# A graph layer with segment maximum on one core: the bytes of the slot stage's temporaries and of the accumulator change places

## The chip, the core and the metric

The kernel runs on one core of one Trainium2 chip. The metric is the device time of one execution in microseconds. The kernel before takes 754.3 us (median of 3 runs, 753.62 to 754.97). One more execution was recorded by the hardware profiler; it took 746.02 us, and all the rows below are from it.

The engines are called as in the profile: PE multiplies matrices, DVE (VectorE) and ACT (ScalarE) work on tiles elementwise, POOL (GpSimd) issues the indirect loads, SP (SyncE) issues most of the direct ones.

## What is computed

```python
e   = relu((x[dst] - x[src]) @ theta_w.T + theta_b + x[src] @ phi_w.T + phi_b)   # one row per edge
out = segment_max(e, dst, num_segments=6250)        # 0 for a node with no edge
y   = layernorm(x + out)
```

There are 6250 nodes of 256 float32 and 100000 edges, sorted by dst. Since the dst part is the same for all edges of a node, the kernel computes b = x (phi − theta)' once for every node, takes for every node the maximum of b over its sources, adds a = x theta' + biases, and applies relu, residual and normalisation.

## The kernel before, in words

**Stages.** The search (`search_edges`, L621) finds where the nodes' edges lie; a branch (L653) would sort the edges if they weren't sorted. B's stage (L710 to L784) loads the weights and biases (L719, L722), prepares them (L726 to L740), loads x in 13 shares (L775), transposes (L747) and multiplies (L759) on PE with copies on ACT (L749, L762), and stores b in DRAM as `b_rows`. The end stage (from L1292) multiplies x by theta, joins it with the maxima and normalises.

**Two ways to the maxima.** The first 1130 nodes are done by 146 gather steps: POOL loads one row for each of 128 partitions by an indirect DMA (L512), DVE folds it into the running maximum (L688). 48 of these rows come from x and are multiplied in B's stage (`x_group`, L764), 98 come from `b_rows`. They lie in a ring of 6 tiles `g` of 8 rows.

The other 5120 nodes are done mostly by one-hot matmuls. `b_rows` is cut into 17 slots of 383 rows; for each node and slot a choice (`choice`, L997, on DVE) names one row of the slot, and `wanted` (L1024) stores these names as `chosen_rows` in DRAM, two slots at a time. `slot_terms` (L1039) loads a slot's rows into `raw` (one buffer), and makes two terms of them: a cast on ACT (L1053) and the difference on DVE (L1054). `slot_part` (L1056) does one slot for one chunk of 1024 nodes: it loads `want` from `chosen_rows` (L1061), makes one-hot rows of it, one block of 128 rows on DVE (L1065, once `dve_hots` is 1) and the others on ACT (L1067, L1068), does 24 matmuls (L1075; 8 in the last slot) in two halves, and joins each half with the accumulator `acc`: a copy on ACT for slot 0 (L1084), a maximum on DVE (L1086) for the other 16 slots. There are 85 such parts.

What a slot can't name goes to a list: `list_pieces` (L1167) packs the left-over edges to the front of a table of 1440 words in moves by powers of two (L1200, L1203), tags them (L1208, L1209), stores them in DRAM as `list_words` (L1210), loads them again from where each partition's run begins (three gathers `dst_w`, by `gather_run`, L521) and makes `list_src` and caps of them (L1221 to L1235). Then 232 list gathers (`gather_2`, L1260) go through POOL, and DVE folds them in by L688 too, and stores of `maxima` follow.

**What sets the order.** The program is written stage by stage, but a planner puts the instructions of each engine in the order in which it expects them to be ready. It must keep data dependences, and also those by place: a tile whose pool was opened where an earlier pool had been closed can't be written before the earlier tiles' readers are done. `behind_in_order` adds an order of two instructions without a wait; POOL's gathers are held in the written order in this way (`in_turn`, L506), and the list's L688 behind the latest L1086 (L694).

**What the change touches.** The pool `accs` with `acc` (L703, L704) is opened ahead of B's stage, the pools `work` (heads, owner, `hot_1` and other small tiles) and `slots` (`raw`, `terms`, `want`, `hot`, `rows`) behind it (L786, L787), where the pools of B's stage, `prep`, `x_in` and `b_out`, have just been closed. The sort's and the search's pools were closed ahead of these (L648, L662). In `slot_terms` the three or four row loads (L1045, L1047, L1051) are issued without any order of their own.

Of the kernel before, what the change touches and what calls it, by code (L numbers as in the profile page):

```python
# [40 lines left out]
FP = mybir.dt.float32  # L41
# [11 lines left out]
P = 128  # L53
# [45 lines left out]
def flat(t, offset, ap):  # L99

    return bass.AP(tensor=t.tensor, offset=t.offset + offset, ap=ap)
# [326 lines left out]
def gnn_kernel(ctx: ExitStack, tc: tile.TileContext, x, src, dst, theta_w, theta_b, phi_w, phi_b, out):  # L428
    nc = tc.nc
    N, D = x.shape  # L430
    E = src.shape[0]
    T = -(-E // P)
    KC = D // P
    OWN = P * TILES
# [20 lines left out]
    body = ctx.enter_context(ExitStack())  # L455
    ps_misc = body.enter_context(tc.tile_pool(name="ps_misc", bufs=2, space=PSUM))

    b_rows = dram.tile([N, D], FP, name="b_rows")
    maxima_1 = dram.tile([P * T1 + 1, D], FP, name="maxima_1")
    maxima_2 = dram.tile([P * LIST + 1, D], FP, name="maxima_2")  # L460
# [12 lines left out]
    def shares(width):  # L473

        main = ((1, Q1), (2, TILES))
        return [LAST] + [(part, j, min(width, n - j)) for part, n in main for j in range(0, n, width)]

    def node_rows(t, part, j0, n):
        if (part, j0, n) == LAST:
            return t[P * Q1 : N1, :].rearrange("p (o d) -> p o d", o=1)  # L480
        base, tiles = (0, Q1) if part == 1 else (N1, TILES)
        return flat(t, (base + j0) * D, [[tiles * D, P], [D, n], [1, D]])

    def present(t, part, j0, n):
        return t[: LEFT1 if (part, j0, n) == LAST else P, :n, :]
# [16 lines left out]
    def behind_in_order(one, name, reason):  # L502
        after = mybir.DependencyInfo(mybir.DependencyClass.NoSync, mybir.DependencyReason.DATA)
        tc.add_manual_dep(one.ins, name, after, reason=reason)
# [49 lines left out]
    whole = [[E // P, P], [1, E // P]]  # L554
    rest = [[E % P, 1], [1, E % P]]
# [142 lines left out]
    def run_1(i, gathers=()):  # L698
        t0, n = groups[i]
        run(1, ring_tiles[i], n, caps_1, t0, maxima_1t[:, t0 : t0 + n, :], gathers)  # L700


    acc_pool = body.enter_context(tc.tile_pool(name="accs", bufs=1))  # L703
    acc = acc_pool.tile([P, KC, OWN], FP, name="acc")  # L704

    weights = const.tile([P, KC, 2, D], FP, name="weights")

    bias_terms = const.tile([P, D], FR, name="bias_terms")
# [1 line left out]
    with (  # L710
        tc.tile_pool(name="prep", bufs=1) as prep,
        tc.tile_pool(name="x_in", bufs=4) as x_in,
        tc.tile_pool(name="b_out", bufs=2) as b_out,
        tc.tile_pool(name="ps_t", bufs=3, space=PSUM) as ps_t,
        tc.tile_pool(name="ps_b", bufs=3, space=PSUM) as ps_b,
    ):
        w_in = prep.tile([P, 2, KC, D], FP, name="w_in")
        for i, w in enumerate((phi_w, theta_w)):
            nc.sync.dma_start(w_in[:, i], w.rearrange("(c p) k -> p c k", p=P))  # L719
        biases = prep.tile([P, 2, D], FP, name="biases")  # L720
        for i, b in enumerate((theta_b, phi_b)):
            nc.sync.dma_start(biases[:, i, :], flat(b, 0, [[0, P], [1, D]]))  # L722
        bias = prep.tile([P, D], FP, name="bias")
        rest = prep.tile([P, D], FP, name="rest")
        high_part = prep.tile([P, D], FR, name="high_part")
        nc.vector.tensor_add(bias, biases[:, 0, :], biases[:, 1, :])  # L726
        nc.vector.tensor_copy(high_part, bias)
        nc.vector.tensor_tensor(rest, bias, high_part.bitcast(FP), op=ALU.subtract)
        nc.vector.tensor_scalar(bias, high_part.bitcast(FP), ident[:, 0:1], None, op0=ALU.mult)
        nc.vector.scalar_tensor_tensor(bias_terms, rest, ident[:, 1:2], bias, op0=ALU.mult, op1=ALU.add)  # L730
        pick_one = prep.tile([P, 1], FP, name="pick_one")
        nc.vector.tensor_add(pick_one, ident[:, 0:1], ident[:, 1:2])
        nc.vector.tensor_copy(pick, pick_one.to_broadcast([P, P]))
        nc.vector.tensor_sub(w_in[:, 0], w_in[:, 0], w_in[:, 1])
        for i in range(2):
            for c in range(KC):
                ps = ps_t.tile([P, 2, KC, P], FP, name="ps_xt")
                for k in range(KC):
                    nc.tensor.transpose(ps[:, 0, k, :], w_in[:, i, c, k * P : (k + 1) * P], ident)
                nc.vector.tensor_copy(weights[:, :, i, c * P : (c + 1) * P], ps[:, 0])  # L740

        def x_transposed(rows):
            w = rows.shape[1]
            ps = ps_t.tile([P, 2, KC, P], FP, name="ps_xt")
            for h in range(w):
                for k in range(KC):
                    nc.tensor.transpose(ps[:, h, k, :], rows[:, h, k * P : (k + 1) * P], ident)  # L747
            x_t = prep.tile([P, 2, KC, P], FP, name="x_t", bufs=3)
            nc.scalar.copy(x_t[:, :w], ps[:, :w])  # L749
            return x_t  # L750

        def b_of(to, rows):

            n = rows.shape[1]
            x_t = x_transposed(rows)
            ps = ps_b.tile([P, 2, D], FP, name="ps_b")
            for h in range(n):
                for k in range(KC):
                    nc.tensor.matmul(  # L759
                        ps[:, h, :], x_t[:, h, k, :], weights[:, k, 0, :], start=(k == 0), stop=(k == KC - 1)  # L760
                    )
            nc.scalar.copy(to, ps[:, :n, :])  # L762

        def x_group(i):  # L764
            for q in range(0, STEPS, 2):
                rows = ring_tiles[i][:, q : q + 2, :]
                b_of(rows, rows)
            run_1(i)

        for k, share in enumerate(shares(4)):  # L770
            n = share[2]
            x_q = x_in.tile([P, 4, D], FP, name="x_q")
            if share == LAST:
                nc.vector.memset(x_q[:, 0, :], 0.0)
            nc.sync.dma_start(present(x_q, *share), node_rows(x, *share))  # L775
            b_sb = b_out.tile([P, 4, D], FP, name="b_sb")
            for i in range(0, n, 2):
                w = min(2, n - i)
                b_of(b_sb[:, i : i + w, :], x_q[:, i : i + w, :])
            nc.scalar.dma_start(node_rows(b_rows, *share), present(b_sb, *share))  # L780
            if k == X_AFTER:
                x_group(of_x[0])
        for i in of_x[1:]:
            x_group(i)  # L784

    work = body.enter_context(tc.tile_pool(name="work", bufs=2))  # L786
    slots = body.enter_context(tc.tile_pool(name="slots", bufs=2))  # L787
    fetch = body.enter_context(ExitStack())
    ps_fetch = fetch.enter_context(tc.tile_pool(name="ps_fetch", bufs=3, space=PSUM))

# [7 lines left out]
    first = const.tile([P, 1], FP, name="first")  # L798
# [190 lines left out]
    def rows_in(s):  # L989

        return min(SLOT_ROWS, N - s * SLOT_ROWS)

    def blocks_in(s):

        return rows_in(s) // P + 1
# [38 lines left out]
    raw = slots.tile([P, KB, D], FP, name="raw", bufs=1)  # L1034
# [4 lines left out]
    def slot_terms(s):  # L1039

        first, left, n = s * SLOT_ROWS, rows_in(s), blocks_in(s)
        whole = n - 1
        rest = left % P
        if whole:
            nc.sync.dma_start(raw[:, :whole, :], flat(b_rows, first * D, [[D, P], [P * D, whole], [1, D]]))  # L1045
        if left < SLOT_ROWS:
            nc.sync.dma_start(raw[rest : rest + 1, whole, :], maxima_2[0:1, :])  # L1047
        even = rest // 16 * 16
        for a, b in ((0, even), (even, rest)):
            if b > a:  # L1050
                nc.sync.dma_start(raw[a:b, whole, :], flat(b_rows, (first + whole * P + a) * D, [[D, b - a], [1, D]]))  # L1051
        terms = terms_of[s] = slots.tile([P, PARTS, KB, D], FR, name="terms")
        nc.scalar.copy(terms[:, 0, :n], raw[:, :n])  # L1053
        nc.vector.tensor_tensor(terms[:, 1, :n], raw[:, :n], terms[:, 0, :n].bitcast(FP), op=ALU.subtract)  # L1054

    def slot_part(s, c):  # L1056
        if c == 0:
            slot_terms(s)
# [428 lines left out]
```

## Time and profile before

| | |
|---|---|
| timed runs | 754.3 us (753.62 to 754.97, 3 runs) |
| profiled execution | 746.02 us |
| its span, which all rows are counted in | 744.2 us |
| granted TensorE clock, mean | 0.955 |
| B's stage on PE (L747, L759) | 34.23 to 147.6 us |
| first and last one-hot matmul (L1075) | 165.13 and 652.6 us |
| b_rows gathers of the first part (POOL, 98) | 111.94 to 275.4 us |
| list gathers (POOL, 232) | 277.18 to 633.46 us |
| end stage on PE | from 654.38 us |

A row of a group reads: line, engine, operation, tile written and tiles read with their sizes, number of instructions; behind the first bar the busy time in us and the mean ns of one; behind the second the idle time of the engine just before them and what ended most of it. A row of a timeline reads: start and length in us, engine, line, operation, tiles, number; in brackets the idle time before it and what released it. "issue" means that the engine waited for nothing that the profile shows.

### The profile page before, as it was taken

The numbers are of one execution on the slowest core, as the hardware profiler recorded it, in microseconds if no ns is written. First come the engines' busy times: TensorE is split into PE (matmuls) and PEld (weight loads), VectorE is DVE, ScalarE is ACT, GpSimd is POOL, SyncE is SP. The second block draws the span as 40 slices with busy tenths as digits, with TensorE's granted clock in tenths as the row PEclk, the third lists the DMA queues.
The fourth block names the chain that finished last, engine by engine and source line by source line (L and its number), as shares of the span: only waits on it lengthen the run. The fifth ranks groups of instructions, "written<-read, shape, count | busy, mean of one in ns | idle before, by whom it ended". The sixth has DMA issues, their size and how long they took to land.

```text
span 744.2 us, 10255 instructions
## 1 busy us (share of the span) xinstructions
PE 650.4 (87%) x3018; PEld 537.3 (72%) x3018; DVE 641.4 (86%) x1197; ACT 492.7 (66%) x700; POOL 604.9 (81%) x843
## 2 busy tenths in 40 slices
PE   1299999939777999999999999999999999589970
PEld 0288888726556788688888888888888888479970
DVE  6699999999997989598889989889799899768871
ACT  0144444459997777688777877877787775037885
POOL 7788987788887778888888888888888888648840
PEclk9599999959999999999999999999999999999995
DMA  6577745584677787968777777768768777625542
GB/s 207 144 244 244 248 159 193 176 286 151 209 239 256 239 254 231 356 211 267 230 235 223 261 243 251 228 223 251 262 205 261 229 222 250 224 101 180 180 173 116
DMA packets 55895, 164.84 MB, mean 221 GB/s; under 512 B 11835, under 2 KB 19796, under 8 KB 48500
## 3 DMA queue, kind: packets, MB, share of 16 engines
q1 hardware_dynamic: 32344, 98.76, 38.1%
q0 software_dynamic: 20944, 57.62, 27.5%
q10 hardware_dynamic: 2540, 7.69, 2.9%
q8 instruction: 27, 0.44, 0.3%
q14 instruction: 40, 0.33, 0.1%
HBM read 101.08 MB, written 63.74 MB: 221 GB/s over the span
## 4 chain that ended last, share of the span: by engine, by line
PE 52%; ACT 11%; DVE 5%; DMA 5%; POOL 3%; issue 2%; DVEq 0%; ACTq 0%; POOLq 0%; SPq 0%
PE ps_f L1075 49%; DMA want<-chosen_rows 4%; POOL g L512 3%; ACT x_f L1338 3%; ACT squares L1328 3%; ACT hot L1067 2%; ACT hot L1068 2%; DVE acc L1086 2%; PE ps_e L1299 1%; ACT acc L1084 1%; DMA g<-b_rows,src 1%; ACT x_t L1294 1%; DVE g L688 1%; DVE x_f L1314 1%; DVE g L1310 0%
## 5 line engine op out<-in xcount | busy, mean ns | idle before, releaser
L1075 PE MATMUL ps_f<-hot,terms 128*128 128x512 f32 x1960 | 458.0, 395 | 29.0 <-ACT hot L1068 15.6
L1075 PEld LDWEIGHTS ps_f<-hot,terms 128*128 128x128 f32 x1960 | 370.2, 190 | 113.1 <-ACT hot L1068 19.8
L512 POOL DMA_INDIRECT g<-b_rows,list_src x232 | 235.4, 1015 | 39.4 <-issue 35.6
L1067 ACT ACTIVATE hot<-want,minus_row 128x1024 fp32r<-128x1024 f16 x169 | 186.2, 1147 | 92.7 <-PE ps_f L1075 80.2
L1086 DVE TENSOR_TENSOR acc<-acc,ps_f 128x1024 f32<-128x1024 f32 x160 | 193.5, 1215 | 31.9 <-PE ps_f L1075 31.0
L688 DVE SCALAR_TENSOR_TENSOR g<-g,caps 128x256 f32<-128x256 f32 x376 | 180.0, 479 | 8.4 <-DMA g<-b_rows,src 5.2
L1068 ACT ACTIVATE hot<-hot 128x1024 fp32r<-128x1024 f32 x169 | 169.1, 1046 | 0.0
L512 POOL DMA_INDIRECT g<-b_rows,src x98 | 128.0, 1306 | 30.5 <-issue 25.3
L488 POOL IOTA pause<- 128x160 f32 x384 | 120.4, 314 | 5.5
L759 PE MATMUL ps_b<-weights,x_t 128*128 128x256 f32 x388 | 90.5, 388 | 1.3 <-ACT x_t L749 0.5
L759 PEld LDWEIGHTS ps_b<-weights,x_t 128*128 128x128 f32 x388 | 72.9, 192 | 14.4 <-ACT x_t L749 5.0
L512 POOL DMA_INDIRECT g<-in_x_dram,src x48 | 60.3, 1256 | 11.3 <-issue 7.1
L512 POOL DMA_INDIRECT g<-maxima,place x49 | 47.6, 972 | 24.6 <-issue 22.5
L1065 DVE TENSOR_SCALAR hot<-want,row_id 128x1024 fp32r<-128x1024 f16 x76 | 59.8, 788 | 6.4 <-DMA want<-chosen_rows 6.3
L1299 PE MATMUL ps_e<-weights,x_t 128*128 128x256 f32 x192 | 48.5, 380 | 0.3 <-ACT x_t L1294 0.2
L1299 PEld LDWEIGHTS ps_e<-weights,x_t 128*128 128x128 f32 x192 | 32.8, 190 | 3.9 <-ACT x_t L1294 0.8
L1294 ACT COPY x_t<-ps_e 128x512 f32<-128x512 f32 x24 | 13.7, 574 | 32.4 <-PE ps_e L1292 32.4
L762 ACT COPY b_sb<-ps_b 128x512 f32<-128x512 f32 (+1 forms) x25 | 14.4, 578 | 29.8 <-PE ps_b L759 28.0
L762 ACT COPY g<-ps_b 128x512 f32<-128x512 f32 x24 | 14.1, 586 | 29.8 <-PE ps_b L759 27.5
L1338 ACT ACTIVATE x_f<-x_f,r 128x256 f32<-128x256 f32 x49 | 25.3, 590 | 10.8 <-DVE r L1335 10.7
L749 ACT COPY x_t<-ps_xt 128x512 f32<-128x512 f32 (+1 forms) x49 | 26.1, 593 | 0.0
L1328 ACT ACTIVATE squares<-x_f,r 128x256 bf16<-128x256 f32 x49 | 24.2, 499 | 1.6 <-DMA g<-b_rows,list_src 1.0
(266 smaller groups left out, 502.2 us busy)
## 6 DMA issues: line engine op xcount, KB each, us to landing
maxima<-g SPq DMA_DIRECT2D x47, 1024.0 KB
want<-chosen_rows SPq DMA_DIRECT2D x85, 256.0 KB
x_q<-in_x_dram SPq DMA_DIRECT2D x12, 512.0 KB
b_rows<-b_sb ACTq DMA_DIRECT2D x12, 512.0 KB
x_f<-in_x_dram SPq DMA_DIRECT2D x5, 1024.0 KB
out_dram<-x_f SPq DMA_DIRECT2D x5, 1024.0 KB
raw<-b_rows SPq DMA_DIRECT2D x16, 256.0 KB
g<-b_rows,list_src POOLq DMA_INDIRECT x232, 4.3
```

Source lines behind the costliest of these rows:

```text
L488: return nc.gpsimd.iota(t, pattern=[[step, t.shape[1]]], base=base, channel_multiplier=per_partition, allow_small_or_imprecise_dtypes=True,)
L512: in_turn(nc.gpsimd.indirect_dma_start(out=out, out_offset=out_offset, in_=in_, in_offset=in_offset))
L688: one = nc.vector.scalar_tensor_tensor(g[:, k, :], last[part], caps[:, t : t + 1], g[:, k, :], op0=ALU.min, op1=ALU.max)
L759: nc.tensor.matmul(ps[:, h, :], x_t[:, h, k, :], weights[:, k, 0, :], start=(k == 0), stop=(k == KC - 1))
L1065: nc.vector.tensor_scalar(hot[:, b, :], want, row_id[:, b : b + 1], None, op0=ALU.is_equal)
L1067: nc.scalar.activation(hot[:, b, :], want, AF.Abs, bias=minus_row[:, b : b + 1], scale=1.0)
L1068: nc.scalar.activation(hot[:, b, :], hot[:, b, :].bitcast(FP), AF.Relu, bias=1.0, scale=-1.0)
L1075: nc.tensor.matmul(ps[:, w : w + 512], terms[:, part, b, h * P : (h + 1) * P], hot[:, b, w : w + 512], start=(i == 0), stop=(i == n - 1),)
L1086: latest_part[0] = nc.vector.tensor_tensor(to, to, ps, op=ALU.max).ins.name
L1299: nc.tensor.matmul(a[:, i, :], x_t[:, 2 * i + c, :], weights[:, c, 1, :], start=(c == 0), stop=False)
L1328: nc.scalar.activation(squares, x_f[:, k, :], AF.Square, bias=mean[:, k : k + 1], scale=1.0, accum_out=var[:, k : k + 1])
L1338: nc.scalar.activation(x_f[:, k, :], x_f[:, k, :], AF.Identity, bias=mean[:, k : k + 1], scale=inv[:, k : k + 1])
```

## The change

The pools `work` and `slots` are opened where `accs` was, and `accs` where they were. So the temporaries of the slot stage have bytes of their own while B's stage runs, and `acc` lies where the tiles of B's stage lay. The sizes of all tiles and the number of buffers are as before. The row loads of a slot are collected in `pieces` and then issued; those of slot 0 are put in SP's order behind the last load of x.

```diff
-    acc_pool = body.enter_context(tc.tile_pool(name="accs", bufs=1))
-    acc = acc_pool.tile([P, KC, OWN], FP, name="acc")
-
+    work = body.enter_context(tc.tile_pool(name="work", bufs=2))
+    slots = body.enter_context(tc.tile_pool(name="slots", bufs=2))
     weights = const.tile([P, KC, 2, D], FP, name="weights")
...
-            nc.sync.dma_start(present(x_q, *share), node_rows(x, *share))
+            x_loaded = nc.sync.dma_start(present(x_q, *share), node_rows(x, *share)).ins.name
...
-    work = body.enter_context(tc.tile_pool(name="work", bufs=2))
-    slots = body.enter_context(tc.tile_pool(name="slots", bufs=2))
+    acc_pool = body.enter_context(tc.tile_pool(name="accs", bufs=1))
+    acc = acc_pool.tile([P, KC, OWN], FP, name="acc")
     fetch = body.enter_context(ExitStack())
...
+        pieces = []
         if whole:
-            nc.sync.dma_start(raw[:, :whole, :], flat(b_rows, first * D, [[D, P], [P * D, whole], [1, D]]))
+            pieces.append((raw[:, :whole, :], flat(b_rows, first * D, [[D, P], [P * D, whole], [1, D]])))
         if left < SLOT_ROWS:
-            nc.sync.dma_start(raw[rest : rest + 1, whole, :], maxima_2[0:1, :])
+            pieces.append((raw[rest : rest + 1, whole, :], maxima_2[0:1, :]))
         even = rest // 16 * 16
         for a, b in ((0, even), (even, rest)):
             if b > a:
-                nc.sync.dma_start(raw[a:b, whole, :], flat(b_rows, (first + whole * P + a) * D, [[D, b - a], [1, D]]))
+                pieces.append((raw[a:b, whole, :], flat(b_rows, (first + whole * P + a) * D, [[D, b - a], [1, D]])))
+        for to, rows in pieces:
+            one = nc.sync.dma_start(to, rows)
+            if s == 0:
+                behind_in_order(one, x_loaded, "x ahead of a slot's rows")
```

## The prediction

> **What bounds the kernel now.** I read the page first (busy shares, chain, groups), then the chain in order of time, then the timelines of the engines at the places where the chain changes hands. Parts and gathers are counted as the code issues them: a part is one slot by one chunk (24 matmuls, L1075, two halves that VectorE folds in at L1086); there are 146 first-part gathers and then 232 list gathers, each folded in by one L688.
>
> ```profile
> PE 650.4 (87%) x3018; PEld 537.3 (72%) x3018; DVE 641.4 (86%) x1197; ACT 492.7 (66%) x700; POOL 604.9 (81%) x843
> L1075 PE MATMUL ps_f<-hot,terms 128*128 128x512 f32 x1960 | 458.0, 395 | 29.0 <-ACT hot L1068 15.6
> L512 POOL DMA_INDIRECT g<-b_rows,list_src x232 | 235.4, 1015 | 39.4 <-issue 35.6
> L688 DVE SCALAR_TENSOR_TENSOR g<-g,caps 128x256 f32<-128x256 f32 x376 | 180.0, 479 | 8.4 <-DMA g<-b_rows,src 5.2
> ```
>
> Three engines are above 80%, and each has one long group. L1075's 29.0 us of idle lie early: PE has no gap from 248.06 to 635.24 (1556 matmuls at 0.227 us, 5.45 us a part). POOL's 232 list gathers wait for nothing but "issue": 1.535 us each, 277.18 to 633.46. Which of the two chains ends last? The lag between a list gather's issue and its L688 tells: 38.7 us for gather 147, 25 at 450 us, 18.8 at 605, 12.7 at 623.3, 10.3 for gather 368 and 8.1 for gather 370. A list gather lands 4.3 us (median) after issue. So PE ends last, but POOL is only 10.3 − 4.5 = 5.8 (gather 368) to 8.1 − 4.5 = 3.6 us (gather 370) behind. **Any gain of PE beyond 4 to 6 us is lost, unless POOL's list stage starts earlier too, and if that starts over 4 to 6 us later, it sets the end.**
>
> The tail behind those gathers is one chain in VectorE's order (timeline of DVE, then the chain):
>
> ```profile
> 632.15 0.48 DVE L688 SCALAR_TENSOR_TENSOR g<-g,caps 128x256 f32<-128x256 f32 x1
> 632.54 0.15 DVE L1335 TENSOR_TENSOR r<-r 128x1 f32<-128x1 f32 x1
> ...
> 637.06 0.83 DVE hot L1065
> 637.89 0.14 issue
> 638.02 1.18 PE ps_f L1075 x4
> ```
>
> PE's 2.6 us before 638.02 and 5.47 before 647.40 are waits for this VectorE order: a late L688 at 632 delays all the rest to 744.2 one for one.
>
> **What starts POOL's list stage.** Timelines of SP, POOL and DVE:
>
> ```profile
> 219.34 0.34 SPq L1210 DMA_DIRECT2D list_words<-work  x1
> ```
> ```profile
> 257.91 0.95 POOL L512 DMA_INDIRECT dst_w<-list_words,run_start  x1 [0.30 <-DVE acc L1086]
> ...
> 274.22 1.17 POOL L512 DMA_INDIRECT g<-b_rows,src  x1 [0.30 <-issue]
> 277.18 1.14 POOL L512 DMA_INDIRECT g<-b_rows,list_src  x1 [1.79 <-DVE caps L1235]
> ```
>
> Three gathers read list_words, ten more b_rows gathers follow, then list_src: 277.18 − 257.91 = 19.3 us, of which 1.79 is a wait for VectorE. Here list_words was stored 38 us before it was read: free.
>
> **The change part by part** (order of instructions from the two programs; no instruction is added or removed).
>
> *1. Loads and preparation in front of the search: gain.* Weights and biases no longer lie over the search's bytes, so L719/L722 go ahead of it. Before, they were issued at 25.02 to 26.48 and PE waited for them:
>
> ```profile
> 30.82 1.51 PE L739 MATMUL ps_xt<-ident,w_in 128*128 128x128 f32 x6 [15.36 <-DMA biases<-in_L_gnn_phi_b_dram]
> ```
>
> The 15.36 us cannot all go: the branch on unsorted edges stands ahead of L739 (VectorE was past it at 21.73). B's stage starts at 22 to 24, 7 to 9 earlier, and ends near 139 to 141 for 147.6. Price: VectorE's preparation (eight instructions, about 3 us) goes ahead of the choice; its wait for the weights stands ahead of the search, and with it POOL's first gathers at 26.68. I take 1 to 2 us there; bounds: 0 (the idle 3.06 us before 25.03 covers it) to 3.
>
> *2. Slots' tiles beside B's stage: gain.* Slot 0's row loads stand right behind the last x load, terms (L1053, L1054) and the hots of parts 0 and 1 are made inside B's stage. Before, PE stopped at B's end for VectorE's hot and ScalarE's:
>
> ```profile
> 154.52 0.83 PE L825 MATMUL ps<-ids,hot 128*128 128x148 f32 x2 [6.88 <-DVE hot L823]
> 165.13 1.22 PE L1075 MATMUL ps_f<-hot,terms 128*128 128x512 f32 x2 [2.85 <-ACT hot L1068]
> ```
>
> First L1075: 141 to 149 for 165.13, 16 to 24 earlier. ScalarE gets 2 parts x 3 blocks x (1.15 + 1.05) = 13.2 us of hots inside B's stage; the slices there show it at 4 to 5 tenths, so there is room; where B's x_t copies (L749) wait behind them for a want load, B ends up to 4 later (a want load's landing), which item 3 covers.
>
> *3. Where that gain stops.* From part 9 on, VectorE makes the first hot block, and its place is behind the L688 of gather 110 (232 us before), that of part 10 behind gather 114. Those wait for POOL:
>
> ```profile
> 237.80 0.48 DVE L688 SCALAR_TENSOR_TENSOR g<-g,caps 128x256 f32<-128x256 f32 x1 [0.94 <-DMA g<-b_rows,src]
> ```
>
> In all 5.2 us of such waits at 227 to 241. Summing VectorE's row durations, it would be 9 to 12 us ahead at gather 79, meets POOL at gather 100 (212 to 218) and is then bound to it. So PE stands idle from about 212 to 232, starts part 9 at 232 and part 10 at 238.5, where before part 10 started at 248.06: PE is 9.5 us ahead, not 20. POOL's gathers keep their order; part 1 makes them 0 to 2 later.
>
> *4. The list's words: loss.* VectorE's last three moves (L1200/L1203 with 1312, 1184 and 288 columns) and L1208, L1209 stood behind gather 99 and two L1086; now they stand behind gather 127 and 17 L1086, since the parts have moved ahead of them. From 237.8 VectorE's queue to L1209 sums to 25.1 us: nine L1086 at 1.13, six hots at 0.66, two L1054, four pairs of moves (0.7 + 1.45, 0.22 + 0.38), eleven L688 at 0.40 and small ones. L1209 ends at 263 to 265 (floor: the ninth L1086 needs PE's parts 9 to 12 and half of 13, 232 + 4 × 5.45 + 2.74 = 256.5, so 258). The store (144 KB; SP then has one row load and one want ahead of it, 0.5 us each) lands 2.5 to 5 later (want loads 4, place gathers 3.0): list_words is there at 266 to 269 for a POOL that comes at about 257.9. Then 17.5 to 19.3 us to the first list gather: 283.5 to 288. **POOL's list stage is 6.5 to 11 late; I take 7.5** (the low side, because the third dst_w gather can land while the ten b_rows gathers run); bounds: 0 if POOL finds the words there, +12 with 5 us on top.
>
> From gather 145 on VectorE's order is the same as before, with PE 9.5 ahead and POOL 7.5 behind: the lag of 38.7 becomes 22, and that of 12.7 at gather 360 would be −4.3: POOL overtakes as the bound around gather 330. **Sum at the tail:** −5.8 to −3.6 (POOL's slack) + 7.5 = +1.7 to +3.9; with the low store −0.5 less. I take **+2.0**: 748.0 for the profiled 746.02 (span 744.2 and 1.8 around it), which is 8.3 below the median of the timed runs; by ratio 754.3 × 1.0027 = **756.3**.
>
> **The Trainium skill against this.** The rows first: POOL's gathers take 0.95 us alone; the six from 202.77 to 213.86, beside the moves of 1376 to 288 columns, took 2.86, 1.59, 0.96, 2.02, 2.13 and 1.07, 4.9 us over 6 × 0.95. Those beside L1086 (222.40 to 228.67) took 0.94 to 0.96. The Trainium skill, "GPSIMD Engine Reference", section Specifications, says that GpSimd shares its SBUF interfaces with VectorE and contends with instructions that have two SBUF inputs; the trace agrees for the long moves, hardly for L688 (two SBUF inputs, gathers of 0.97 to 1.14 beside five of them at 219.74). What the rows alone give is the third rival.
>
> **Rivals.**
> - *The words are not late (not slower).* If VectorE is not held at gathers 100 to 115, or reaches L1209 by 255, POOL comes to list_words no later, and the end moves by POOL's slack alone: −3.6 to −5.8, about 749.5 by the median. It decides if the first list gather starts before 277.18 + 3.6 = 280.8. For it: part 4 rests on a sum of 25 us with a floor at 258; against: the 5.2 us of waits show that POOL binds there. Chance 0.25.
> - *More late.* Preparation costs POOL 3 us and the moves stretch gathers next to the ten b_rows ones: list stage +12, so +6 to +8: 761. Chance 0.13.
> - *The moved long instructions free the gathers.* The 4.9 us go from gathers 100 to 105, gather 115 lands at 233 to 235, L1209 ends at its floor 258 to 260, POOL's list stage is 3.5 to 5.5 late: −2 to +1.5, no change, 754. Chance 0.22.
> - *The forecast:* 0.40, 754.5 to 758.5.
>
> **Chances and range.** Less than 0.2% (1.5 us) cannot be told from no change. Faster: 0.25 and a quarter of the third rival, 0.31. Same: the rest of the third and a quarter of the forecast, 0.26. Slower: the rest of the forecast and "more late", 0.43. The range 748.5 to 761.5 leaves out a gain above 5.8 and the far end of "more late".
>
> **What would show it.** Right: L739 before 25; L1075 near 145; PE idle before 232; L1209 behind 258; a wait for list_words ahead of dst_w; first list gather at 283 to 288; lags at gathers 360 to 370 down to 4 to 6. Wrong: a first list gather at 277 or before, or lags above 8 at the end with PE still ahead.

## The result, and the profile after

The changed kernel takes 758.43 us (median of 20 runs, 754.73 to 762.73) against 753.61 us (median of 20, 746.55 to 757.71): ratio 1.0086, 95% interval 1.0065 to 1.0107, so slower by 0.86%. The profiled execution took 758.03 us, its span is 756.2 us. The ratio compares fast executions alone and is worth 753.6 × 0.0086 = 6.5 us; the two medians lie 4.8 us (0.64%) apart. The two profiled spans are 12.0 us apart: the profiled execution of the kernel before was one of its shortest. The rows below show where time went, and the runs how much of it is usual.

From words_early_2 on, the runs were made on other chips, on which the kernel before took 800 and 805 us and engines stand still for more than 10 us at once with no wait that the profile can name (31.0 us in one of them), so neither their ratios nor their single waits can be set beside the rows of the first chip without care.

Lines of the kernel after are 4 higher from `slot_part` on (L1079 for L1075, L1090 for L1086, L1214 for L1210) and one lower in B's stage (L738 for L739). The page, for the groups that the prediction began with:

```profile
PE 654.2 (87%) x3018; PEld 542.2 (72%) x3018; DVE 640.2 (85%) x1197; ACT 491.8 (65%) x700; POOL 612.4 (81%) x843
L1079 PE MATMUL ps_f<-hot,terms 128*128 128x512 f32 x1960 | 463.7, 398 | 44.3 <-DVE hot L1069 30.4
L688 DVE SCALAR_TENSOR_TENSOR g<-g,caps 128x256 f32<-128x256 f32 x376 | 181.0, 481 | 27.0 <-DMA g<-b_rows,src 12.3
L512 POOL DMA_INDIRECT g<-b_rows,src x98 | 135.8, 1386 | 30.0 <-issue 24.7
```

Busy times hardly moved; the waits did. PE waits 30.4 us for VectorE's hots (its largest wait before was for ScalarE's), VectorE 12.3 us for b_rows gathers (5.2 before), and the 98 gathers themselves take 135.8 us instead of 128.0.

The start, from the timelines of DVE and PE:

```profile
7.56 0.69 DVE L733 TENSOR_TENSOR w_in<-w_in 128x512 f32<-128x512 f32 x1 [3.08 <-DMA w_in<-in_L_gnn_theta_w_dram]
...
14.61 2.97 DVE L728 TENSOR_SCALAR bias<-high_part,ident 128x256 f32<-128x256 f32 x1
...
23.05 0.15 DVE L640 TENSOR_SCALAR window<-counts 128x1 int32<-128x1 f32 x1
```
```profile
26.75 1.51 PE L738 MATMUL ps_xt<-ident,w_in 128*128 128x128 f32 x6 [4.92 <-DVEq L653]
```

The preparation stands ahead of the search as foreseen. But the search's last instruction (L640) comes at 23.05 instead of 17.59, 5.5 us later. New ahead of it are waits of 3.08 and 1.56 us for the weights and biases and one tensor_scalar of 2.97 us (the kernel before has one as long at that time, L810, 2.73 us at 14.40, but not ahead of the search's hot); gone is a wait of 2.24 us for POOL's `columns` at 10.75. PE begins with the weights (L738) 4.1 us earlier, but then waits 3.60 us for VectorE's copies of them, so that the first x (L746) is transposed at 32.34 instead of 34.23, only 1.9 us earlier; and POOL's gather 7 is issued at 26.3 instead of 20.8.

The middle, from the timelines of PE and POOL:

```profile
239.21 7.49 PE L1079 MATMUL ps_f<-hot,terms 128*128 128x512 f32 x24 [17.88 <-DVE hot L1069]
248.63 11.65 PE L1079 MATMUL ps_f<-hot,terms 128*128 128x512 f32 x43 [1.94 <-DVE hot L1069]
```
```profile
278.88 0.94 POOL L512 DMA_INDIRECT dst_w<-list_words,run_start  x1 [7.76 <-DVE g L688]
...
297.16 0.95 POOL L512 DMA_INDIRECT g<-b_rows,list_src  x1 [0.30 <-DVE g L688]
```

The first one-hot matmul starts at 153.54 (165.13 before), 11.6 us earlier; then PE waits 17.88 us for the hot of part 9, and part 10 starts at 248.63, where it started at 248.06 before. **In this execution the head start is gone at part 10.** The list's words are stored at 273.52 (219.34 before), POOL waits 7.76 us ahead of dst_w, and the first list gather is issued at 297.16, 20.0 us later than before. From SP's timeline, and from POOL's of `pools_only` (an experiment below):

```profile
273.52 0.34 SPq L1214 DMA_DIRECT2D list_words<-work  x1
```
```profile
288.83 0.95 POOL L512 DMA_INDIRECT dst_w<-list_words,run_start  x1 [8.41 <-DMA list_words<-work]
```

That POOL waits for the words is read from `pools_only`, where the profile names them. In the kernel after it names a VectorE instruction that ended just before, but there too dst_w goes out 5.4 us behind the store (4.3 us in `pools_only`).

The tail is the chain in order of time; it now runs through POOL, where it ran through PE:

```profile
628.97 0.96 POOL g L512
630.38 0.95 POOL g L512
631.79 6.18 DMA g<-b_rows,list_src
638.06 0.48 DVE g L688
```

A table of L688 by number, in us, tells the two losses apart (from the timelines of DVE and POOL; `after_no_pause` and `prep_late` are experiments below):

| | before | after | prep_late | after_no_pause |
|---|---|---|---|---|
| gather 7 (POOL) | 20.8 | 26.3 | 22.2 | 26.0 |
| gather 93 (POOL) | 187.2 | 201.8 | 200.4 | 197.8 |
| L688 number 113 | 231.4 | 240.4 | 233.9 | 234.2 |
| L688 number 129 | 261.4 | 278.3 | 272.0 | 271.4 |
| first list gather (POOL) | 277.2 | 297.2 | 290.4 | 290.4 |
| L688 number 149 | 321.3 | 326.4 | 320.2 | 320.5 |
| L688 number 353 | 614.7 | 620.3 | 615.2 | 615.0 |
| L688 number 365 | 627.1 | 640.5 | 633.4 | 627.3 |
| span | 744.2 | 756.2 | 753.3 | 741.0 |

From number 149 to 353 VectorE has the same order in both kernels and PE sets its pace: +5.1 to +5.6 us in the kernel after. Between 353 and 365 another 7.8 us come, where POOL becomes the bound. 5.6 + 7.8 = 13.4, of which 12.0 are left at the end. The two columns on the right have the changed order too, but not the first loss (0.5 and 0.3 us at number 353); prep_late, which keeps the pauses, has 5.8 us of the second.

### The profile page after: what moved, and what is told of

Read it like the earlier page. It is cut to its first block, busy times and chain, and to the rows that moved or that the text cites. A ratio compares the mean times of both kernels' runs of the same rounds, so it can differ in the third digit from the quotient of the medians.

```text
span 756.2 us, 10247 instructions
## 1 busy us (share of the span) xinstructions
PE 654.2 (87%) x3018; PEld 542.2 (72%) x3018; DVE 640.2 (85%) x1197; ACT 491.8 (65%) x700; POOL 612.4 (81%) x843
## 4 chain that ended last, share of the span: by engine, by line
PE 47%; DVE 11%; ACT 10%; POOL 8%; DMA 7%; issue 6%; SPq 0%; DVEq 0%; ACTq 0%; POOLq 0%
PE ps_f L1079 40%; POOL g L512 7%; PE ps_b L758 4%; ACT x_f L1342 3%; ACT squares L1332 3%; DMA g<-b_rows,src 2%; DVE g L688 2%; DVE acc L1090 2%; PE ps_e L1303 1%; ACT hot L1071 1%; DMA want<-chosen_rows 1%; ACT hot L1072 1%; ACT acc L1088 1%; DMA out_dram<-x_f 1%; DMA g<-b_rows,list_src 1%
## 5 line engine op out<-in xcount | busy, mean ns | idle before, releaser
L1079 PE MATMUL ps_f<-hot,terms 128*128 128x512 f32 x1960 | 463.7, 398 | 44.3 <-DVE hot L1069 30.4
L1079 PEld LDWEIGHTS ps_f<-hot,terms 128*128 128x128 f32 x1960 | 374.8, 192 | 129.0 <-issue 32.1
L512 POOL DMA_INDIRECT g<-b_rows,list_src x232 | 234.2, 1009 | 37.9 <-issue 36.0
L1090 DVE TENSOR_TENSOR acc<-acc,ps_f 128x1024 f32<-128x1024 f32 x160 | 193.8, 1215 | 29.8 <-PE ps_f L1079 29.3
L688 DVE SCALAR_TENSOR_TENSOR g<-g,caps 128x256 f32<-128x256 f32 x376 | 181.0, 481 | 27.0 <-DMA g<-b_rows,src 12.3
L512 POOL DMA_INDIRECT g<-b_rows,src x98 | 135.8, 1386 | 30.0 <-issue 24.7
L758 PE MATMUL ps_b<-weights,x_t 128*128 128x256 f32 x388 | 92.2, 392 | 5.6 <-ACT x_t L748 5.0
L758 PEld LDWEIGHTS ps_b<-weights,x_t 128*128 128x128 f32 x388 | 73.9, 195 | 19.4 <-ACT x_t L748 9.8
L512 POOL DMA_INDIRECT g<-in_x_dram,src x48 | 62.3, 1298 | 11.5 <-issue 6.9
L512 POOL DMA_INDIRECT g<-maxima,place x49 | 47.8, 975 | 18.6 <-issue 16.5
```

What stands on the lines that cost most here:

```text
L512: in_turn(nc.gpsimd.indirect_dma_start(out=out, out_offset=out_offset, in_=in_, in_offset=in_offset))
L688: one = nc.vector.scalar_tensor_tensor(g[:, k, :], last[part], caps[:, t : t + 1], g[:, k, :], op0=ALU.min, op1=ALU.max)
L758: nc.tensor.matmul(ps[:, h, :], x_t[:, h, k, :], weights[:, k, 0, :], start=(k == 0), stop=(k == KC - 1))
L1079: nc.tensor.matmul(ps[:, w : w + 512], terms[:, part, b, h * P : (h + 1) * P], hot[:, b, w : w + 512], start=(i == 0), stop=(i == n - 1),)
L1090: latest_part[0] = nc.vector.tensor_tensor(to, to, ps, op=ALU.max).ins.name
```

## The experiments

Theory A: the preparation ahead of the search delays every gather, the list's words come late, and POOL's list stage, delayed by both, sets the end. Rival B: the loss is PE's alone, through the late hots of parts 9 and 10. Rival C: the gathers stretched beside VectorE's long moves are the loss. Rival D came up with after_no_pause: with POOL's list stage out of the way the change is a gain.

**prep_late.** The preparation (eight VectorE instructions) is ordered behind the search; the loads stay where they are.

```diff
-        nc.vector.tensor_scalar(window, counts[:, 0:1], float(E - WINDOW), None, op0=ALU.min)
+        found.append(nc.vector.tensor_scalar(window, counts[:, 0:1], float(E - WINDOW), None, op0=ALU.min).ins.name)
...
-        nc.vector.tensor_add(bias, biases[:, 0, :], biases[:, 1, :])
+        behind_in_order(nc.vector.tensor_add(bias, biases[:, 0, :], biases[:, 1, :]), found[0], "the search first")
```

> The changed kernel, but VectorE's eight instructions of weight and bias preparation are ordered behind the last instruction of the search (window). Theory A (preparation ahead of the search delays every gather, and late list words delay the list gathers; POOL's list stage then sets the end): the gathers behind the branch start at 20.8 instead of 26.3 us, first list gather at 290 to 293 instead of 297, end 4 to 6 us earlier than the changed kernel, ratio to the kernel before 1.000 to 1.004. Rival B (the loss is PE's: parts 9 and 10 held by VectorE's hots, POOL has no part in it): end within 1 us of the changed kernel, 1.008.

Measured: 755.61 us against 750.99, ratio 1.0065 (1.0037 to 1.0093). The search is back (L642 at 17.29), gather 7 is at 22.2, the first list gather at 290.39 as expected, and PE's chain is back too: +0.5 at number 353. Neither can be credited to the edit: after_no_pause, below, keeps the preparation ahead of the search and has 290.44 and +0.3. The delay also returns soon, as gather 13 is issued at 39.4 for 34.5 before. And the list stage stays late:

```profile
272.14 1.16 POOL L512 DMA_INDIRECT dst_w<-list_words,run_start  x1 [5.46 <-DVE n_bad L1462]
...
290.39 1.02 POOL L512 DMA_INDIRECT g<-b_rows,list_src  x1 [0.30 <-issue]
```

POOL still waits 5.46 us for words stored at 267.19, and its list stage is still 13.2 us late, so number 365 is 6.3 us late. In the profiled pair the edit is worth 2.9 us, in the ratios 0.0021 with intervals that overlap: less than expected, and as a gain not proven by the times. Theory A's first half, that the preparation ahead of the search delays the list, is thus not shown.

**words_early.** The list's words are to be tagged at gather 100, as in the kernel before: later L688 and maxima are ordered behind the tag.

```diff
+        tag = nc.vector.tensor_tensor(done, done, owner.to_broadcast([P, OWN_LIST]), op=ALU.bitwise_or).ins.name
+        for one in runs[100:] + joins[8:]:
+            behind_in_order(one, tag, "the list's words first")
```

> The changed kernel, but every L688 from the 101st on and every maximum with the accumulator from the 9th on is ordered behind the instruction that tags the list's words, so that the words are stored as early as gather 100. Theory A: POOL's 7.8 us of waiting ahead of dst_w go, first list gather at 288 to 290, end 5 to 8 us earlier than the changed kernel, ratio 0.998 to 1.002. Rival B: PE's parts are not earlier, 1.006 to 1.010. Rival C (the gathers stretched beside VectorE's long moves are the loss): no gain either, 1.008.

Measured: 762.72 us, ratio 1.0156 (1.011 to 1.0202), slower than the changed kernel. POOL did come to dst_w without a wait, at 269.10, and the first list gather was issued at 292.44 (288 to 290 expected), but the planner put the instruction that uses dst_w far ahead too (timeline of DVE):

```profile
247.91 0.48 DVE L689 SCALAR_TENSOR_TENSOR g<-g,caps 128x256 f32<-128x256 f32 x1
273.37 0.46 DVE L1238 COPY_PREDICATED dst_w<-words,dst_w 128x266 int32<-128x266 int32 x1 [24.98 <-DMA dst_w<-list_words,run_start]
```

It waits 24.98 us at the head of VectorE's queue, and every L688 and every maximum stands behind it: number 109 comes at 275.2 (235.7 in the kernel after), PE is 15 us late at number 353. Both the time and the ratio were missed. The run says nothing for or against the theory, since the wait that it takes from POOL came back, larger, on VectorE.

**both_early.** Both edits.

> Both edits at once. Theory A: first list gather at 282 to 285, the end 9 to 13 us earlier than the changed kernel, ratio 0.993 to 0.998, so faster than the kernel before. If the two delays lie beside each other and do not add: only as good as the better one alone, 0.998 to 1.002. Rival B: 1.006 to 1.010.

Measured: 759.93 us, ratio 1.012 (1.008 to 1.0161). The same wait (26.26 us here), the same 15 us at number 353 (629.4). Missed for the same reason.

**after_no_pause.** The pauses behind the list gathers go (`paced[0] = 1` becomes `0`).

> The changed kernel with no pause instruction behind each list gather. A list gather then takes about 1.25 instead of 1.535 us, so POOL's list stage ends over 40 us earlier. Theory A, which says that POOL sets the tail: the tail's 6 to 8 us of waiting for list gathers go, ratio 0.999 to 1.002, and what stays over the kernel before is the 5 us that PE is late between 320 and 600 us. Rival B: no change, 1.008.

Measured: 747.53 us, ratio 0.9963 (0.9932 to 0.9994): 1.0086 − 0.9963 = 0.0123, or 9 us, under the changed kernel, more than was expected. POOL is through with the list at 608, and the tail waits for no gather; it is again the chain that the kernel before has:

```profile
637.29 0.68 DVE hot L1069
637.97 0.14 issue
638.10 1.18 PE ps_f L1079 x4
639.46 5.21 DMA want<-chosen_rows
```

638.10 for 638.02 before. So in the changed kernel POOL's list stage sets the end (without the pauses it moves), and PE's order, freed from it, ends where it ended before. That refutes rival B, which expected no change. The program of after_no_pause is that of the changed kernel up to the list stage on every engine; yet its first list gather comes at 290.44, 6.7 us earlier than in the changed kernel's profiled execution, and number 353 5.3 us earlier. So those 5 to 7 us of the changed kernel's profile are spread between executions, not a fixed cost. That also holds for the gain of prep_late at number 353. The 5 to 7 us arise at gathers 88 to 97, which take 34.2 us in the kernel after and 23.1 us here (24.1 before): rival C's stretch, but not in each execution.

The same trace shows where PE's head start goes when that stretch is absent (timelines of PE and DVE):

```profile
232.29 8.22 PE L1079 MATMUL ps_f<-hot,terms 128*128 128x512 f32 x24 [13.38 <-DVE hot L1069]
241.64 5.72 PE L1079 MATMUL ps_f<-hot,terms 128*128 128x512 f32 x24 [1.13 <-DVE hot L1069]
...
279.88 21.43 PE L1079 MATMUL ps_f<-hot,terms 128*128 128x512 f32 x82 [4.03 <-DVE hot L1069]
```
```profile
276.71 0.46 DVE L1226 COPY_PREDICATED dst_w<-words,dst_w 128x266 int32<-128x266 int32 x1 [4.79 <-DMA dst_w<-list_words,run_start]
```

Part 10 starts at 241.64, 6.4 us ahead of the kernel before (242.17 in prep_late). Then VectorE stands 4.79 us for the dst_w rows (2.30 in the kernel before), the hot of part 16 stands behind that, and PE waits 4.03 us for it: part 17 starts at 288.0, where it started at 286.3 before. So the late words cost PE its head start as well as POOL its slack.

**words_early_2, both_early_2.** As words_early and both_early, with the use of dst_w held behind the 132nd L688. These and the next two runs are from a chip on which the kernel before took 805 us.

```diff
+            joined.append(nc.vector.copy_predicated(list_edges, mask, to))
...
+                    if joined and len(runs) == 132:
+                        for later in joined:
+                            behind_in_order(later, one.ins.name, "the runs first")
```

> As words_early (words tagged and stored at gather 100), but the two instructions that use the dst_w rows, for which VectorE waited 25 us there, are held behind the 132nd L688. Theory A: no such wait, POOL does not wait ahead of dst_w either, first list gather at 286 to 291, the tail gets 5 to 8 us back, PE is still about 5 us late at 350 us: ratio 1.000 to 1.004. If early words cost as much in VectorE's order (moves ahead of the L688 of gathers 100 on) as POOL gains: 1.006 to 1.010.

> words_early_2 and the preparation behind the search. Theory A: both losses are gone, first list gather at 281 to 286, PE as in the kernel before at 350 us, ratio 0.996 to 1.002. If the stretched gathers beside the moves are what is left, POOL is still 5 us late without any wait: first list gather at 286 to 290, ratio 1.002 to 1.006.

Measured: 808.29 us, ratio 1.0109 (1.0048 to 1.017), and 811.15 us (790.43 to 814.18) against 804.77 (792.07 to 809.47), too spread for a ratio. Both missed their first list gather: 326.64 for 286 to 291, and 301.03 for 281 to 286. These are POOL's timeline in both_early_2, and the row of the first list gather in both_no_pause (below), which has the same order up to there:

```profile
262.37 0.95 POOL L512 DMA_INDIRECT dst_w<-list_words,run_start  x1 [0.30 <-issue]
...
301.03 0.94 POOL L512 DMA_INDIRECT g<-b_rows,list_src  x1 [21.62 <-DVE caps L1258]
```
```profile
297.13 0.94 POOL L512 DMA_INDIRECT g<-b_rows,list_src  x1 [15.94 <-DVE caps L1258]
```

POOL is at dst_w at 262.37, 16.5 us earlier than in the kernel after, and without a wait; then it waits 21.62 us for caps. That is not a clean price: 14.0 us of VectorE's time in this stretch are waits of this chip's kind (3.67 for nothing named, 3.84 that the profile calls remote, 6.50 for a PE that stands still itself). In both_no_pause VectorE waits only 5.1 us there, all for PE, POOL is at dst_w at 263.75, and it still waits 15.94 us for caps. VectorE makes the last of these behind 25 maxima (19 in the kernel before, 23 in the changed one), and it comes to them only when PE has done the parts of those maxima; the use of dst_w is moreover held behind the 132nd L688 by the edit itself. Early words alone don't start the list in this order. The theory's second half is thus too narrow: the wait for the words is one of several places at which the list's preparation now stands behind the parts.

**before_no_pause, pools_only.** The kernel before without pauses; the changed kernel without the order of slot 0's row loads behind x.

```diff
-    paced[0] = 1
+    paced[0] = 0
```
```diff
-            if s == 0:
-                behind_in_order(one, x_loaded, "x ahead of a slot's rows")
```

> The kernel before without the pauses behind the list gathers. It tells what after_no_pause (0.9963) owes to the pauses alone. Theory A (the kernel before is bound by PE's order, POOL's list stage has some us of slack and its runs differ by how much of it is left): 0.992 to 0.998, and the changed kernel without pauses is 0 to 3 us above it. Rival D (with POOL's tail out of the way the change is the gain that was wanted): no change, 0.999 to 1.001, so that the changed kernel without pauses is 3 us below it.

> The changed kernel without the order that puts slot 0's row loads behind the last x load; the pools stay where the change puts them. Theory A: the loss comes from the bytes alone, 1.006 to 1.011, as the changed kernel. If the forced order is what makes it late: below 1.003; if it protects x: over 1.012.

Measured: before_no_pause 905.72 us against 804.77, ratio 1.1269 (1.1178 to 1.1361). pools_only 798.04 us (783.85 to 812.80) against the same 804.77: too spread for a ratio, inconclusive. In pools_only the row loads of the first slots go between x loads, and POOL waits 8.41 us ahead of dst_w all the same (the row shown above). The words are tagged behind 17 maxima and 127 L688 there as in the changed kernel (2 and 99 in the kernel before), so that place in the order comes from the bytes alone; what the forced order is worth in time isn't settled. before_no_pause missed by far: 0.992 to 0.998 was expected.

**The second tries.** They are both_early_2, before_no_pause and words_early_2 again, and both_early_2 without pauses; they fell on another chip, where the kernel before took 800 us.

> both_early_2 again, since the kernel before took 805 us beside it, with stalls of 10 to 25 us in which engines waited for nothing that the profile shows. Theory A: first list gather at 281 to 286, PE as in the kernel before at 350 us, ratio 0.996 to 1.002. If the stretched gathers beside the moves are what is left: first list gather at 286 to 290, ratio 1.002 to 1.006.

> before_no_pause again, for the same reason. Theory A: 0.992 to 0.998 (the pauses cost the kernel before some us too). Rival D (the change is a gain once POOL's tail is out of the way): 0.999 to 1.001, against 0.9963 for the changed kernel without pauses.

> words_early_2 again, for the same reason. Theory A: no wait of POOL ahead of dst_w, first list gather at 286 to 291, PE 5 us late at 350 us, ratio 1.000 to 1.004. If early words cost as much in VectorE's order as POOL gains: 1.006 to 1.010.

> both_early_2 without the pauses behind the list gathers: the candidate for a kernel faster than both. Theory A: PE's order alone sets the end; as the changed kernel without pauses (0.9963) or up to 3 us better, 0.992 to 0.997. If POOL's list stage still bound both_early_2: as before_no_pause_b.

Measured: both_early_2b 810.82 us (795.51 to 817.32) and words_early_2b 808.87 us (792.55 to 816.16) against 799.86 (790.43 to 815.29), too spread for ratios; before_no_pause_b 903.15 us, ratio 1.1312 (1.1216 to 1.1408); both_no_pause 910.52 us, ratio 1.1476 (1.1394 to 1.1557). The wait for caps was there again, 22.11 us in both_early_2b and 26.29 us in words_early_2b, with 15.3 and 17.8 us of VectorE's waits in it, most of them called remote. None of the four came out as theory A expected. Rival D can't be judged: there is no run of the kernel before without pauses on the chip where the changed kernel without them gained.

## Why the prediction was right, and which terms were off

**Sign and mechanism.** "If that starts over 4 to 6 us later, it sets the end" is what came: the list stage starts 20.0 us later in the profiled execution and the chain of the tail runs through POOL's list gathers; after_no_pause shows that it is POOL's list stage that holds the end. The forecast +2.0 us (0.27%) is a third of the measured 0.86%. The term that was too small is the fourth, the list stage "6.5 to 11 late; I take 7.5": it was 13.2 us late in prep_late, 13.3 in after_no_pause and 20.0 in the profile after. The sum around it held: with 13.2 it gives +7.4 to +9.6, and the span of prep_late is 9.1 us over the kernel before.

**A reading that came out by luck.** The lag of 38.7 us was to become 22 with PE 9.5 ahead and POOL 7.5 late; in the profile after it is 24.4, with VectorE and PE 5.1 us *behind* and POOL 19.4 late. Two misses cancel in it. The lags of the tail, 4 to 6 expected, are 3.6 to 6.8 at gathers 352 to 373. (Counted one by one, the lags of 38.7, 10.3 and 8.1 in the prediction are those of gathers 150, 371 and 373, and from 248.06 to 635.24 PE runs 1688 matmuls with two waits of 0.31 and 1.14 us; nothing hangs on either.)

**Part 1, preparation.** "I take 1 to 2 us there; bounds: 0 to 3": measured 5.5, outside the bounds. The sum named the wait for the weights and gave it no time of its own; two instructions wait for DMAs at the head of the queue (3.08 and 1.56 us), and one ran long (2.97 us). The gain was smaller too: L738 at 26.75, not 22 to 24, since the branch came later by what the search lost, and the 3.60 us for the weights' copies were not in the sum. What the 5.5 us cost further on isn't seen: after_no_pause has them as well, and its list stage is no later than that of prep_late, which hasn't.

**Part 2, the slots' tiles.** First L1079 at 153.54 for "141 to 149" (148.79 in prep_late). B's last matmuls end at 152.9, not "139 to 141", although its first x is transposed 1.9 us earlier: ScalarE's x_t copies made PE wait 5.0 us, ScalarE itself waited 4.3 us for `raw` (waits up to 160 us). B's end is 5 us later than before, and "up to 4 later, which item 3 covers" is right in kind: PE waited 17.88 us at part 9 anyway.

**Part 3, where the gain stops.** The hots of parts 9 and 10 held PE at the two places named (behind the 111th and 115th L688 in the trace's count). The times came in the executions without the long stretch: part 9 at 232.29 in after_no_pause and 232.77 in prep_late (232 forecast), part 10 at 241.64 and 242.17 (238.5 forecast), so PE was 6 us ahead there for the 9.5 forecast. In the profile after, POOL's gathers were not "0 to 2 later" but 9 to 10 at that place (L688 number 113: 240.4 for 231.4; 2.5 and 2.8 us late in the other two), so part 9 started at 239.21, part 10 at 248.63, and PE was 0.6 behind. What the forecast lacked in all three is the step after it: VectorE's wait for the dst_w rows (4.1 to 4.8 us, 2.30 before) and PE's behind it. At number 353 PE is 0.3 us behind in after_no_pause: the 12.7 us of head start at its first one-hot matmul are worth nothing from there on.

**Part 4, the words.** The tag ended at 273.5 (263 to 265 expected), in after_no_pause at 266.5 and in prep_late at 267.2; store to dst_w took 5.4 us (2.5 to 5 expected). From dst_w to the first list gather 18.3 us (17.5 to 19.3 expected). So the structure held. What failed is "a POOL that comes at about 257.9": start less wait, POOL was through with the gathers ahead of dst_w at 265.4 in after_no_pause, 266.7 in prep_late and 271.1 in the profile after. The words were then 5.5 to 7.8 us later still. Part of POOL's delay is new: the last moves lie beside gathers 116 to 136 now, which take 24.8 to 26.8 us instead of 21.6.

**The rivals.** "The words are not late" is refuted: they were late in each profiled execution of the changed order (7.76, 7.09, 5.46 and 8.41 us of POOL's wait). "The moved long instructions free the gathers" did not come: the 98 gathers took 135.8, 132.5 and 129.2 us (the profile after, prep_late, after_no_pause) instead of 128.0, so the stretch moved and, in some executions, grew. "More late" (list stage +12) is nearest to the prep_late and after_no_pause executions (13.2 and 13.3), also in its reason that moves stretch late gathers, and its end of +6 to +8 is what the ratio says (6.5 us); it had a chance of 0.13.

**The stretched gathers.** The rows: in the kernel after, a first-part gather, by what VectorE runs in its first 0.95 us, takes beside an L1090 and nothing else over 0.6 us 1.03 us (mean of 15), beside another instruction of 1.3 us or more 2.66 us (mean of 13, the longest 9.07), beside one of 0.6 to 1.3 us 1.39 us (mean of 40, the longest 5.24), beside short ones or none 1.01 us (mean of 30); in the kernel before 1.02, 2.14 (longest 3.75), 1.26 and 1.00. The timelines of POOL and DVE show the longest one beside three of the list's moves:

```profile
185.38 9.07 POOL L512 DMA_INDIRECT g<-b_rows,src  x1 [0.31 <-issue]
```
```profile
184.56 1.88 DVE L1207 COPY_PREDICATED work<-words,work 128x1439 int32<-128x1439 int32 x1
...
187.88 1.86 DVE L1207 COPY_PREDICATED work<-words,work 128x1438 int32<-128x1438 int32 x1
...
191.17 1.89 DVE L1207 COPY_PREDICATED work<-words,work 128x1436 int32<-128x1436 int32 x1
```

The rule of the Trainium skill ("GPSIMD Engine Reference", Specifications) that GpSimd contends with VectorE's instructions of two SBUF inputs agrees with the rows of the long moves, and shows little in those of L688, which has two as well and is among the short ones. What the rows add is how long one gather can be held: 9.07 us in the kernel after, 9.04 in prep_late and 9.06 in words_early, each time a gather that begins beside the move of 1439 columns. In after_no_pause, with the same order, three gathers of 3.05, 3.00 and 2.28 us lie beside these moves. The long one needs no changed order: the kernel before has 3.75 us at most in its profile, but 9.08 and 9.75 in before_no_pause and before_no_pause_b, on the other chips. Why one execution has it and another has not stays open.

**What stays open.** How much of the 6.5 us is the search, how much the late words and how much the stretched gathers isn't split by times: prep_late takes 0.0021 of the ratio, within its interval, and the rows of single executions differ by 6.7 us at the first list gather. No variant removed the late list alone, because each order forced on one step made VectorE or POOL wait at the next. Whether the changed kernel without pauses beats the kernel before without pauses isn't known.

## What to carry to other kernels

Where a planner orders the queues, giving tiles bytes of their own moves every instruction that had waited for the old bytes; ask of each moved instruction which DMA it waits for and who stands behind it in its queue, since that wait can be far more than its duration (24.98 us for 0.46 in words_early). In this case a head start on an engine that later waits for another engine's stream was worth nothing; follow the slower stream (here POOL's gathers) and count what the change does to its start. A step whose result has 38 us of slack can lose all of it to instructions that moved ahead of it, so list the slack of each producer that the new order passes. One profiled execution can carry a delay that the next has not (6.7 us here), so a term is read from more than one before it is put down to the change.

## What the runs showed of the hardware that was not expected

- One indirect gather was held for 9.07 us beside VectorE's long predicated copies, where the same instruction takes 0.95 us alone. Executions of one order differ in this: in after_no_pause no gather beside the same three copies took over 3.05 us. The first list gathers of the two are 6.7 us apart.
- The kernel without pauses behind its list gathers gained on one chip (changed kernel, 0.9963) and lost 12.7% to 14.8% on two others (kernel before and both_no_pause). In before_no_pause_b ScalarE's hots waited 88.6 us and VectorE's maxima 85.7 us for something that the profile calls remote, up to 31.0 us at once. The same chips are slower with pauses too (800 and 805 us for 751 to 754). Whether the chip or the kernel makes the difference wasn't tried, as no kernel without pauses ran on both sorts.
